# A fused layernorm, S4 convolution and NF4 gated MLP: the inverse transform of the S4 kernel with 8 products in place of 12

## The chip, the cores and the metric

The kernel runs on one core of one Trainium2 chip. A core has a tensor engine (PE, with its weight loads shown apart as PEld), a vector engine (VectorE, DVE), a scalar engine (ScalarE, ACT), GpSimd (POOL) and a sync engine (SP) whose queue issues most of the transfers. The metric is the device time of one execution in microseconds, the median of several runs. A change below about 0.2% of this kernel's time is hard to tell from none.

## The reference, cut to what matters

The input x has 4 x 512 rows of 512 features. It is normalised by layernorm, and the output is x plus an S4 convolution of the normalised x plus a gated MLP of it whose weights are 4-bit codes with scales.

```python
xn = _layernorm(x, axis=-1)
x = x + _L0_attn_ref(xn, ...) + _L0_ffn_ref(xn, ...)

# in _L0_attn_ref -> _s4_kernel
Omega = jnp.exp(-2j * jnp.pi * (jnp.arange(L) / L))       # L = 512
...
at_roots = c * (k00 - k01 * (1.0 / (1.0 + k11)) * k10)
return jnp.fft.ifft(at_roots, L).real

# in _L0_attn_ref
y = jnp.fft.irfft(jnp.fft.rfft(u, n=n) * jnp.fft.rfft(K, n=n), n=n)[..., :L]
return y + D[0] * u
```

The change touches the last line of `_s4_kernel`: the real part of an inverse Fourier transform of 512 complex values, which gives the 512 taps of the convolution kernel K.

## The kernel before, in words

**Stages.** The rows come in four blocks (`tb`) of 512. The first stage loads x, normalises it, transposes it on PE and computes the first pair of gate and up products (lines 499 to 657, an order written out by hand for ScalarE, VectorE, PE and SP). Then, for each m from 1 to 13, the codes of 128 gate and 128 up columns are dequantised by ScalarE and VectorE (`dequant`, line 237), and `hidden` (line 439) multiplies them with the four blocks on PE: 24 matmuls of 512 columns for a block, 96 for an m, and then a silu on ScalarE (line 432), a gating multiply on VectorE (line 436) and a store by SP (line 437). Every f32 operand of these is split in three parts, so that three products replace one. In between, the S4 part is emitted: `s4_roots` (line 253) after m=2, `s4_toeplitz` (line 366) after m=3, and the convolution `conv` (line 446) of one block after each of m=5 to 8. The last stage, `down` (line 464), multiplies with the down weights, and adds and stores the result.

**The S4 part.** `s4_roots` evaluates the transfer function at the 512 roots. The roots are held as four residues of 128: root 4p + r is partition p, column r. The result is in three tiles of 128 x 4, `qr`, `qi` and `nqi` (real part, imaginary part, minus the imaginary part).

`s4_toeplitz` makes the inverse transform in two steps. The **twist** (lines 377 to 380) multiplies each residue's 128 values by a 128 x 128 table of cosines and sines (`al`, `be`, loaded at line 370) into a real and an imaginary matrix (`ar`, `ai`): four VectorE operations for a residue, 16 in all, each over 128 x 128. Then **the products** (line 388) multiply these, as stationary operands, with a table of cosines and sines `b` of that residue. The table is loaded at line 369 (two blocks of 128 columns for a residue, cosine and minus sine), and GpSimd (line 372) writes its negative beside it, so that four turns by a quarter are at hand. The PSUM tile `pm` has four sums of 128 columns: residue 0, residue 2, and two sums over residues 1 and 3 with different turns. They take 2 + 2 + 4 + 4 = 12 products of 128 x 128 by 128 x 128 in f32. VectorE copies `pm` out, and adds and subtracts the sums (lines 397 to 401) into `toep`, which GpSimd masks (line 402); it is split in three parts into `tp` (line 409), the moving operand of the convolution.

**Buffers.** `b` and `b1` (which holds `al`, `be`, `ar`, `ai`) are the two buffers of the tag "xt", used before by `s4_roots` and after by the convolution's and the last stage's blocks. `pm` is one of four PSUM slots of two banks, which the `hidden` products use in turn.

**Order.** After the hand-ordered first stage, a planner with its own cost estimates orders the instructions of each engine, by the order in which the code emits them and by when it takes their inputs to be ready. Engines then work their queues in order, and wait for one another by semaphores. ScalarE and VectorE instructions emitted up to m=3 are tied behind the first stage (lines 673 to 676).

Of the kernel before, what the change touches and what calls it, by code (L numbers as in the profile page):

```python
# [12 lines left out]
ALU = mybir.AluOpType  # L13
# [3 lines left out]
P = 128  # L17
# [4 lines left out]
L = 512  # L22
# [39 lines left out]
def layernorm_s4_nf4_glu_kernel(  # L62
# [8 lines left out]
    down_s: bass.AP,  # L71
    s4_cols: bass.AP,
    s4_row: bass.AP,
    trig: bass.AP,
    cos_col: bass.AP,
    dft: bass.AP,
# [3 lines left out]
    nc = tc.nc  # L80
    V, S, G, T = nc.vector, nc.scalar, nc.gpsimd, nc.tensor
# [5 lines left out]
    def bank2(name):  # L87
        return psum.tile([P, 2, 512], F32, tag="ps", name=name)

    f = lambda ap: ap.bitcast(F32)  # L90
# [14 lines left out]
    def split(dst, src):  # L105
        S.activation(dst[0], src, AF.Copy, scale=TRIM)  # L106
        V.tensor_tensor(dst[1], src, f(dst[0]), ALU.subtract)  # L107
        V.scalar_tensor_tensor(dst[2], f(dst[1]), -LAM, f(dst[0]), ALU.mult, ALU.add)  # L108
# [257 lines left out]
    def s4_toeplitz():  # L366
        qr, qi, nqi = roots["qr"], roots["qi"], roots["nqi"]
        b, b1 = (work.tile([P, 4, 512], F32, tag="xt", name=f"s4b{k}") for k in range(2))
        nc.sync.dma_start(b[:, 0:4, 0:256], dft)
        nc.sync.dma_start(b1[:, 0:2, :], twist)  # L370

        G.tensor_scalar(b[:, 0:4, 256:512], b[:, 0:4, 0:256], -1.0, None, ALU.mult)
        al, be, ar, ai = (b1[:, j, :] for j in range(4))
        for r4 in range(4):
            c = bass.ts(r4, P)
            o = slice(r4, r4 + 1)
            V.tensor_scalar(ar[:, c], al[:, c], qr[:, o], None, ALU.mult)
            V.scalar_tensor_tensor(ar[:, c], be[:, c], nqi[:, o], ar[:, c], ALU.mult, ALU.add)
            V.tensor_scalar(ai[:, c], al[:, c], qi[:, o], None, ALU.mult)
            V.scalar_tensor_tensor(ai[:, c], be[:, c], qr[:, o], ai[:, c], ALU.mult, ALU.add)  # L380


        pm = bank2("pm")[:, 0, :].rearrange("p (k q) -> p k q", k=4)
        for k, terms in enumerate((((0, 0),), ((2, 0),), ((1, 0), (3, 0)), ((1, 1), (3, 3)))):
            n = 2 * len(terms)
            for i, (r4, turn) in enumerate(terms):
                for part, lhsT in enumerate((ar, ai)):
                    T.matmul(  # L388
                        pm[:, k, :], lhsT[:, bass.ts(r4, P)],
                        b[:, r4, bass.ts((turn + part) % 4, P)],  # L390
                        start=(i == 0 and part == 0), stop=(2 * i + part == n - 1),
                    )
        toep = work.tile([P, L], F32, tag="h", name="toep", bufs=4)
        tk = toep.rearrange("p (k q) -> p k q", k=4)
        cd = b1[:, 0, 0:384].rearrange("p (k q) -> p k q", k=3)
        pq = b1[:, 1, 0:256].rearrange("p (k q) -> p k q", k=2)
        V.tensor_copy(cd, pm[:, 1:4, :])
        V.tensor_tensor(pq[:, 0, :], pm[:, 0, :], cd[:, 0, :], ALU.add)
        V.tensor_tensor(pq[:, 1, :], pm[:, 0, :], cd[:, 0, :], ALU.subtract)
        V.tensor_tensor(tk[:, 0:2, :], pq, cd[:, 1:3, :], ALU.add)  # L400
        V.tensor_tensor(tk[:, 2:4, :], pq, cd[:, 1:3, :], ALU.subtract)
        G.affine_select(
            out=toep[:, 0:P], in_=toep[:, 0:P], pattern=[[1, P]], compare_op=ALU.is_ge,
            fill=0.0, base=0, channel_multiplier=-1,
        )
        V.scalar_tensor_tensor(
            toep[:, 0:P], ident, row[:, 64:65], toep[:, 0:P], ALU.mult, ALU.add
        )
        split([tp[:, i, :] for i in range(3)], toep)
        return tp  # L410
# [89 lines left out]
    start = len(traced)  # L500
# [159 lines left out]
    for m in range(2, NMT - 2):  # L660
        wp[m + 1] = dequant(gu(m + 1))
        for tb in range(NTB):
            hidden(m, tb, wp[m])
        p = {2: 0, 4: 1, 5: 2, 7: 3, 8: 4, 10: 5, 11: 6}.get(m)
        if p is not None:
            down_weights(p)
        if m == 2:
            s4_roots()
        if m == 3:
            toep = s4_toeplitz()  # L670
        if 5 <= m < 9:
            conv(m - 5, toep)
        if m == 3:
            for ins in list(traced[end:]):
                if ins.engine in (S.engine, V.engine):
                    tc.add_manual_dep(ins, last[ins.engine].name, order, reason="after the first tile")
# [27 lines left out]
def _layouts(a):  # L704

    import numpy as np

    def gu_q(q):
        return np.asarray(q).reshape(NMT, P, NC, P).transpose(0, 3, 2, 1).reshape(NMT, P, 512)

    def gu_s(s):
        return (
            np.asarray(s).reshape(NMT, P, NC, 2).transpose(0, 3, 2, 1).reshape(2 * NMT, 512)
        )

    lam, p, q, vc, ct = (
        np.asarray(a[f"L0_attn_{n}_ri"]) for n in ("Lambda", "p", "q", "Vc", "Ct")
    )
    state = np.concatenate(
        [lam, p, ct.reshape(NS, 2), q, vc.reshape(NS, 2 * NS)], axis=1  # L720
    )
    row = [np.asarray(a[f"L0_attn_{n}"]).reshape(-1) for n in ("Bp", "D", "log_step")]

    lr = 4 * np.arange(P)[:, None] + np.arange(4)[None, :]
    half = np.pi * lr / L
    th = 2 * np.pi * ((lr[:, :, None] * np.arange(P)) % L) / L
    tw = np.pi * ((lr[:, :, None] * (1 - 2 * np.arange(P))) % (2 * L)) / L
    f = np.float32
    return {
        "x": np.asarray(a["L0_attn_u"]).reshape(NTOK, HD),  # L730
        "gate_q": gu_q(a["L0_ffn_gate_q"]),
        "up_q": gu_q(a["L0_ffn_up_q"]),
        "down_q": np.asarray(a["L0_ffn_down_q"]).reshape(HD, NMT, P).transpose(1, 2, 0),
        "gate_s": gu_s(a["L0_ffn_gate_absmax"]),
        "up_s": gu_s(a["L0_ffn_up_absmax"]),
        "down_s": np.asarray(a["L0_ffn_down_absmax"]).reshape(HD, 2 * NMT).transpose(1, 0),
        "s4_cols": np.tile(state, (2, 1)),
        "s4_row": np.concatenate(row)[None, :],
        "trig": np.stack([np.sin(half), np.cos(half)]).transpose(0, 2, 1).reshape(2, L).astype(f),
        "cos_col": np.cos(half).astype(f),  # L740
        "dft": np.concatenate([np.cos(th), -np.sin(th)], axis=2).astype(f),
        "twist": (np.stack([np.cos(tw), np.sin(tw)], axis=1) / L).reshape(P, 2, 512).astype(f),
    }


# [21 lines left out]
```

## Time and profile before

| | |
|---|---|
| Median of 3 runs | 521.77 us (521.66 to 521.78) |
| Profiled execution, own time | 521.76 us |
| its span, first to last instruction | 520.0 us |
| granted TensorE clock, mean | 1.000 |
| Transferred | 96.46 MB, mean 185 GB/s |
| Chain that ended last, by engine | PE 96%, DMA 3% |
| on it: gu (line 416), po (481), pc (454), pm (388), pss (322) | 54%, 29%, 6%, 1%, 0% |

Busy time of each engine by stage, from the trace (the S4 transform's products lie in the third row):

| Stretch, us | PE | PEld | DVE | ACT | POOL | DMA share |
|---|---|---|---|---|---|---|
| 46 to 89 (m=1, 2) | 43.0 | 35.6 | 36.4 | 36.6 | 3.1 | 0.41 |
| 91 to 112 (m=3) | 21.0 | 17.4 | 13.5 | 15.6 | 0.0 | 0.62 |
| 112 to 115 (pm) | 3.0 | 2.9 | 1.2 | 3.0 | 0.0 | 0.73 |
| 115 to 158 (m=4, 5) | 43.0 | 35.6 | 22.4 | 40.1 | 0.4 | 0.81 |
| 158 to 254 (conv, m=6 to 8) | 96.0 | 82.7 | 44.3 | 76.5 | 0.8 | 0.65 |
| 254 to 363 (m=9 to 13) | 109.0 | 90.3 | 30.0 | 25.4 | 7.7 | 0.56 |
| 363 to 516 (down) | 153.0 | 125.7 | 71.5 | 27.0 | 1.2 | 0.37 |

How to read it: the profile is of one execution. A row such as `L388 PE MATMUL pm<-s4b,s4b x24` names the line of the code, the engine, the operation, and the tile written and the tiles read; a count and times follow. PE's instructions are pipelined, so their durations overlap. In the chain of work that ended last, each piece begins where the piece that released it ends. The tile name `s4b` stands for both `b` and `b1`.

### The profile page before, as it was taken

The page shows a single profiled execution, that of the slowest core. Times are in us where ns is not written, and L with a number is a line of the kernel's source. Part 1 is how long each engine was busy: PE and PEld are TensorE (multiplying, and loading weights), DVE is VectorE, ACT ScalarE, POOL GpSimd, SP SyncE. Part 2 cuts the span into 40 slices and gives each one's busy share as a digit, 9 for nine tenths or more (in the row PEclk, how much of TensorE's full clock was granted, in tenths as well). Part 3 has the DMA queues.
Part 4 walks back from the last instruction along what each step waited for, and adds up shares of the span by engine and source line. Part 5 has one row for each costly group of instructions (what it writes and reads, how often), then busy time and mean ns, then how long its engine had stood idle before and what let it go on. Part 6 is the DMA issues. An engine that isn't in the chain of part 4 may idle for free.

```text
span 520.0 us, 6138 instructions
## 1 busy us (share of the span) xinstructions
PE 513.7 (99%) x2336; PEld 421.0 (81%) x2336; DVE 259.8 (50%) x353; ACT 264.0 (51%) x326; POOL 19.9 (4%) x34
## 2 busy tenths in 40 slices
PE   8999999999999999999999999999999999999996
PEld 8556888888888888888888888888888888888885
DVE  6989796756545464253522332113545536536412
ACT  7889599599889968895362211102212112121100
POOL 1210002000000000000000000112000000000000
PEclk9999999999999999999999999999999999999999
DMA  8914417849774877755644322699634534524102
GB/s 298 334 36 150 136 46 283 244 142 329 274 245 153 286 246 263 248 178 187 262 164 191 112 101 79 229 348 336 221 122 133 195 118 145 206 97 161 42 1 81
DMA packets 37231, 96.46 MB, mean 185 GB/s; under 512 B 4689, under 2 KB 5585, under 8 KB 34385
## 3 DMA queue, kind: packets, MB, share of 16 engines
q1 hardware_dynamic: 34320, 80.60, 45.2%
q0 software_dynamic: 2592, 15.21, 8.2%
q8 instruction: 18, 0.29, 0.2%
q10 hardware_dynamic: 288, 0.26, 0.2%
q14 instruction: 13, 0.10, 0.1%
HBM read 61.97 MB, written 34.08 MB: 185 GB/s over the span
## 4 chain that ended last, share of the span: by engine, by line
PE 96%; DMA 3%; DVE 0%; SPq 0%; issue 0%
PE gu L416 54%; PE po L481 29%; PE pc L454 6%; PE u L424 3%; PE g L424 2%; DMA q_g1u<-in_up_q_dram 1%; DMA sc_g0u<-in_up_s_dram 1%; PE pt L168 1%; DMA q_g0u<-in_gate_q_dram 1%; PE pm L388 1%; PE pss L322 0%; DVE xo L488 0%; DVE q_g0u L540 0%; SPq L204 0%; SPq L211 0%
## 5 line engine op out<-in xcount | busy, mean ns | idle before, releaser
L481 PE MATMUL po<-wdt,hp 128*128 128x512 f32 x672 | 153.0, 390 | 0.0
L481 PEld LDWEIGHTS po<-wdt,hp 128*128 128x128 f32 x672 | 125.9, 188 | 27.0 <-DVE xo L488 0.9
L436 DVE SCALAR_TENSOR_TENSOR h<-gu,h 128x512 f32<-128x512 f32 x52 | 35.8, 689 | 108.9 <-ACT h L432 108.8
L106 ACT ACTIVATE hp<-hr 128x1024 fp32r<-128x1024 f32 x28 | 29.7, 1060 | 105.2 <-PE po L481 101.3
L432 ACT ACTIVATE h<-gu 128x512 f32<-128x512 f32 x52 | 30.6, 589 | 92.8 <-PE gu L416 92.8
L107 DVE TENSOR_TENSOR hp<-hr,hp 128x1024 fp32r<-128x1024 f32 x28 | 34.3, 1225 | 62.7 <-ACT hp L106 62.7
L108 DVE SCALAR_TENSOR_TENSOR hp<-hp 128x1024 fp32r<-128x1024 f32 x28 | 34.2, 1223 | 0.9
L454 PE MATMUL pc<-tp,xeT 128*128 128x512 f32 (+1 forms) x64 | 20.7, 323 | 0.0
L454 PE MATMUL pc<-tp,xlT 128*128 128x512 f32 (+1 forms) x64 | 20.6, 322 | 0.0
L454 PE MATMUL pc<-tp,xhT 128*128 128x512 f32 (+1 forms) x64 | 20.3, 318 | 0.0
L488 DVE SCALAR_TENSOR_TENSOR xo<-po,xo 128x512 f32<-128x512 f32 x16 | 10.8, 688 | 18.1 <-PE po L481 18.1
L424 PE MATMUL g<-xf,q_g0u 128*128 128x512 f32 (+1 forms) x40 | 14.7, 509 | 0.6 <-ACT xf L171 0.6
L424 PE MATMUL u<-xf,q_g0u 128*128 128x512 f32 x32 | 15.0, 596 | 0.3 <-DVE q_g0u L540 0.3
L424 PEld LDWEIGHTS g<-xf,q_g0u 128*128 128x128 f32 x40 | 7.4, 190 | 7.1 <-issue 4.8
L454 PEld LDWEIGHTS pc<-tp,xhT 128*128 128x128 f32 x64 | 12.2, 190 | 0.8
L454 PEld LDWEIGHTS pc<-tp,xlT 128*128 128x128 f32 x64 | 12.1, 189 | 0.8
L454 PEld LDWEIGHTS pc<-tp,xeT 128*128 128x128 f32 x64 | 12.1, 189 | 0.6
L460 DVE SCALAR_TENSOR_TENSOR xr<-pc,xr 128x1024 f32<-128x1024 f32 x8 | 9.8, 1219 | 5.2 <-PE pc L454 5.2
L142 DVE BATCH_NORM_STATS2 st<-x 128x6 f32<-128x512 f32 x16 | 10.9, 679 | 3.0 <-DMA x<-in_x_dram 3.0
L219 ACT ACTIVATE q_g0u<-q_g0u 128x256 f32<-128x256 f32 (+1 forms) x32 | 10.3, 407 | 1.4 <-DMA q_g0u<-in_gate_q_dram 1.4
L472 POOL DMA_DIRECT2D xo<-rd x4 | 2.3, 585 | 225.3 <-DMA rd<-xr 118.6
L690 POOL DMA_DIRECT2D wdt<-wdd x14 | 7.3, 528 | 94.2 <-issue 94.0
(278 smaller groups left out, 969.2 us busy)
## 6 DMA issues: line engine op xcount, KB each, us to landing
hd<-h SPq DMA_DIRECT2D x56, 256.0 KB, 2.9
hr<-hd SPq DMA_DIRECT2D x28, 512.0 KB, 3.4
wdt<-wdd POOLq DMA_DIRECT2D x7, 1024.0 KB, 6.9
xr<-in_x_dram SPq DMA_DIRECT2D x4, 1024.0 KB, 7.2
rd<-xr SPq DMA_DIRECT2D x4, 1024.0 KB, 4.9
xo<-rd POOLq DMA_DIRECT2D x4, 1024.0 KB, 7.0
out_dram<-xo SPq DMA_DIRECT2D x16, 256.0 KB, 3.4
wdt<-wdd POOLq DMA_DIRECT2D x7, 512.0 KB, 7.7
```

What stands on the lines that cost most here:

```text
L106: S.activation(dst[0], src, AF.Copy, scale=TRIM)
L107: V.tensor_tensor(dst[1], src, f(dst[0]), ALU.subtract)
L108: V.scalar_tensor_tensor(dst[2], f(dst[1]), -LAM, f(dst[0]), ALU.mult, ALU.add)
L142: V.bn_stats(st[:, j, :], xs[tb][:, j, :])
L219: S.activation(w, w if j else w.bitcast(I32), AF.Prelu, scale=scale, bias=bias, alpha=slope)
L416: T.matmul(ps[:, k, :], wp[:, part, k, bass.ts(c, P)], xT[tb][part][:, :, c, :], start=(part == 0 and c == 0), stop=(part == 2 and c == NC ...
L424: T.matmul(ps[:, j.start * P : j.stop * P], w[:, bass.ts(c, P)], xf[tb].rearrange("p j (c q) -> p j c q", c=NC)[:, j, c, :], start=(c == 0 ...
L432: S.activation(h, pg, AF.Silu, scale=unit)
L436: V.scalar_tensor_tensor(h, pu, unit, h, ALU.mult, ALU.mult)
L454: T.matmul(po[:, k, i * P : HD], xT[tb][part][:, jj + k, i, :], toep[:, part, 0 : HD - i * P], start=(i == 0 and part == 0), stop=(i == NC ...
L481: T.matmul(po[j], hp[:, part, k, bass.ts(j, P)], wd(p, part, k), start=(p == 0 and k == 0 and part == 0), stop=(p == NPR - 1 and k == 1 an ...
L488: V.scalar_tensor_tensor(o, po[j], OUT, o, ALU.mult, ALU.add)
```

## The change

Residue 3 is the complex conjugate partner of residue 1: root 4p + 3 reversed in p is 512 - (4p + 1). The tables on the host are laid out anew, so that column 3 holds residue 3 in reversed order, with the sine part of its twist negated. The twist of residue 3 then adds onto the matrices of residue 1 (`to` is the block 1 for r4 = 3), with the signs of a conjugate, in place of writing matrices of its own. With that, the sums over residues 1 and 3 become products of one matrix: `pm` takes 2 + 2 + 2 + 2 = 8 products. The table `b` of residue 3 is neither loaded nor negated, and the third quarter turn isn't needed any more: the load and GpSimd's multiply go over three residues instead of four. The arithmetic count of the twist stays at 16 operations; two of them change from a multiply to a multiply with an added tile.

```diff
-        nc.sync.dma_start(b[:, 0:4, 0:256], dft)
+        nc.sync.dma_start(b[:, 0:3, 0:256], dft)
         nc.sync.dma_start(b1[:, 0:2, :], twist)
 
-        G.tensor_scalar(b[:, 0:4, 256:512], b[:, 0:4, 0:256], -1.0, None, ALU.mult)
+        G.tensor_scalar(b[:, 0:3, 256:512], b[:, 0:3, 0:256], -1.0, None, ALU.mult)
         al, be, ar, ai = (b1[:, j, :] for j in range(4))
         for r4 in range(4):
+            to = bass.ts((0, 1, 2, 1)[r4], P)
             c = bass.ts(r4, P)
             o = slice(r4, r4 + 1)
-            V.tensor_scalar(ar[:, c], al[:, c], qr[:, o], None, ALU.mult)
-            V.scalar_tensor_tensor(ar[:, c], be[:, c], nqi[:, o], ar[:, c], ALU.mult, ALU.add)
-            V.tensor_scalar(ai[:, c], al[:, c], qi[:, o], None, ALU.mult)
-            V.scalar_tensor_tensor(ai[:, c], be[:, c], qr[:, o], ai[:, c], ALU.mult, ALU.add)
+            for dst, s1, s2 in (
+                ((ar, qr, nqi), (ai, qi, qr)) if r4 < 3 else ((ar, qr, qi), (ai, nqi, qr))
+            ):
+                if r4 < 3:
+                    V.tensor_scalar(dst[:, to], al[:, c], s1[:, o], None, ALU.mult)
+                else:
+                    V.scalar_tensor_tensor(
+                        dst[:, to], al[:, c], s1[:, o], dst[:, to], ALU.mult, ALU.add
+                    )
+                V.scalar_tensor_tensor(
+                    dst[:, to], be[:, c], s2[:, o], dst[:, to], ALU.mult, ALU.add
+                )
 
         pm = bank2("pm")[:, 0, :].rearrange("p (k q) -> p k q", k=4)
-        for k, terms in enumerate((((0, 0),), ((2, 0),), ((1, 0), (3, 0)), ((1, 1), (3, 3)))):
-            n = 2 * len(terms)
-            for i, (r4, turn) in enumerate(terms):
-                for part, lhsT in enumerate((ar, ai)):
-                    T.matmul(
-                        pm[:, k, :], lhsT[:, bass.ts(r4, P)],
-                        b[:, r4, bass.ts((turn + part) % 4, P)],
-                        start=(i == 0 and part == 0), stop=(2 * i + part == n - 1),
-                    )
+        for k, (r4, turn) in enumerate(((0, 0), (2, 0), (1, 0), (1, 1))):
+            for part, lhsT in enumerate((ar, ai)):
+                T.matmul(
+                    pm[:, k, :], lhsT[:, bass.ts(r4, P)], b[:, r4, bass.ts(turn + part, P)],
+                    start=(part == 0), stop=(part == 1),
+                )
...
     lr = 4 * np.arange(P)[:, None] + np.arange(4)[None, :]
+    lr[:, 3] = lr[::-1, 3]
...
+    tw = np.stack([np.cos(tw), np.sin(tw)], axis=1) / L
+    tw[:, 1, 3] *= -1.0
...
-        "dft": np.concatenate([np.cos(th), -np.sin(th)], axis=2).astype(f),
-        "twist": (np.stack([np.cos(tw), np.sin(tw)], axis=1) / L).reshape(P, 2, 512).astype(f),
+        "dft": np.concatenate([np.cos(th), -np.sin(th)], axis=2)[:, :3].astype(f),
+        "twist": tw.reshape(P, 2, 512).astype(f),
```

## The prediction

> **What bounds the kernel now.** I read the page's busy shares first, then the chain of work that ended last in order of time, then the waits of the tensor engine, then the single instructions around the changed lines. The busy shares of the page:
>
> ```profile
> PE 513.7 (99%) x2336; PEld 421.0 (81%) x2336; DVE 259.8 (50%) x353; ACT 264.0 (51%) x326; POOL 19.9 (4%) x34
> ...
> PEclk9999999999999999999999999999999999999999
> ```
>
> PE is busy nearly throughout, at full granted clock. The Trainium skill ("Perfetto Trace Analysis", section "Identifying the Most-Contended Engine") warns against reading this as a bound: matmul busy time says little of the distance to the roofline, and the share of the weight loads is the better measure. That speaks against the change. By the 81% of PEld, a fifth of the time might be gaps that take up any saving, and the sum would be 521.77 us again. So the chain has to decide:
>
> ```profile
> 16.53 0.69 DVE q_g0u L540
> ...
> 45.93 43.56 PE gu L416 x192
> 89.50 0.79 PE pss L322 x8
> 90.29 21.92 PE gu L416 x96
> 112.21 2.68 PE pm L388 x24
> 114.89 43.54 PE gu L416 x192
> 158.42 7.62 PE pc L454 x48
> ...
> 363.22 152.87 PE po L481 x672
> ```
>
> Columns are start, length, what. From 17.26 us to 516.10 us every piece is PE, each begins where the one before it ends, and no wait for a DMA or another engine lies between. The waits of PE alone confirm it:
>
> ```profile
> PE warm L532 <- POOL ident masks.py:199: 1.4, 1, 1.4
> PE g L424 <- ACT xf L171: 0.6, 1, 0.6
> PE u L424 <- DVE q_g0u L540: 0.3, 1, 0.3
> ```
>
> All three belong to the first tile, before 46 us. So the 19% without a weight load are stretches in which a 512-column product streams longer than its load, not idle time, and the row is taken over the rule: what leaves PE's queue leaves the end. The transform (tile pm, line 388) is on the chain with 2.68 us, 0.5%.
>
> **What the change removes.** The code has 12 products of 128 columns; the trace has 24 pairs of weight load and matmul for them, two for each f32 product. Eight remain, so 16 pairs, and 8 leave. What is one worth? The duration of a record is the wrong number:
>
> ```profile
> L388 PEld LDWEIGHTS pm<-s4b,s4b x24: 187/192/192, 111.8 to 114.5; 128*128 128x128 f32 x24
> L388 PE MATMUL pm<-s4b,s4b x24: 270/275/275, 112.0 to 114.6; 128*128 128x128 f32 x24
> ```
>
> 8 x 275 ns would be 2.2 us, but 24 x 275 ns is 6.6 us and the stage lasts 2.68: they overlap. What counts is the distance from start to start. In the timeline of PE:
>
> ```profile
> 112.05 2.84 PE L388 MATMUL pm<-s4b,s4b 128*128 128x128 f32 x24
> 114.64 1.17 PE L416 MATMUL gu<-xhT,wp_g4u 128*128 128x512 f32 x4
> ```
>
> The first of 24 starts at 112.05, the last ends at 112.05 + 2.84 = 114.89, so starts at 114.89 - 0.275 = 114.615: 23 distances in 2.565 us, 111.5 ns each. The chain gives 2.68 / 24 = 111.7 ns. The starts of the loads give (114.5 - 111.82) / 23 = 116.5 ns, an upper end, because their first distance is stretched by the long product in front of pm.
>
> The skill ("TensorE: Matmul & The Clock Gate", section "Back-to-back issue gap") would make it smaller: a warm gap of N / 2.4 + 2.5 ns, 55.8 ns for N = 128, or about 81 ns in a sustained stream of loads and matmuls. Its estimates are 8 x 55.8 = 0.45 us and 8 x 81 = 0.65 us. The row is this very instruction in f32 and stands at 111.5, so it decides: **8 x 111.6 = 0.89 us** off PE. I keep 0.45 and 8 x 116.5 = 0.93 for the range.
>
> **What it adds or moves elsewhere.** Two of VectorE's 16 operations of the twist change kind: for residue 3 the first of each pair becomes a multiply-add onto residue 1.
>
> ```profile
> L377 DVE TENSOR_SCALAR s4b<-s4b,qr x4: 278/278/286, 95.4 to 98.7; 128x128 f32<-128x128 f32 x4
> L378 DVE SCALAR_TENSOR_TENSOR s4b<-s4b,nqi x4: 339/342/344, 96.0 to 99.2; 128x128 f32<-128x128 f32 x4
> ...
> L372 POOL TENSOR_SCALAR s4b<-s4b x1: 3079/3079/3079, 84.3 to 84.3; 128x1024 f32<-128x1024 f32 x1
> ```
>
> 2 x (342 - 278) = 0.13 us. The last four operations now also build on each other's output, in two chains of two. The nearest row is this line itself, where a multiply-add already follows the product it accumulates onto; starts lie 0.2 to 0.34 us apart there, so another 0 to 0.3 us. The block now ends at 99.76 + 0.35 = 100.11 us and pm starts at 112.05: 11.9 us of cover, filled by the products of m=3. Take 0. Were the cover gone, the price would be 0.13 to 0.43 us. Behind the block on VectorE is the gating multiply of line 436 at 102.94, after 2.83 us of idle time in which it waits for ScalarE; that idle time takes the delay too.
>
> GpSimd negates 768 columns in place of 1024: 3.08 x 3/4 = 2.31 us, ending about 86.6 in place of 87.4. That is 25 us ahead of pm: 0. The load of the cosine table shrinks from 512 to 384 KB; it is issued on SP at 80.22 and lands 3.9 us later, so it too is hidden by 25 us or more. Behind it on SP is the load of gate codes for m=5 at 80.93, wanted by ScalarE at 97: 0 either way. The number of transfers stays, and none is moved past another by the diff. The host-side reordering of residue 3 changes contents, not sizes.
>
> **What is late next.** After pm everything on PE comes 0.89 us sooner, so all that PE consumes must have that much to spare. The weights of m=4 are ready at 93.25 + 1.21 = 94.5 us and first used at 114.64: 20 us. Those of m=5 have 24 us (112.5 against 136.5), and the later ones more. The Toeplitz parts are ready at 119.36 + 0.69 = 120.05 and first used at 158.3: 38 us. They will come hardly sooner, because the copy out of pm (114.93) stands behind a gating multiply that starts at 114.33 once ScalarE has delivered, whenever pm ends; the cover is ample all the same. PSUM has four slots: that of the first m=4 product is read out by 122.65 and wanted again at 136.5, 14 us. From 254 us on the other engines wait for PE, and the waits move with it.
>
> **The sum.** Against the profiled execution's own 521.76 us (span 520.0, 1.76 us around it): 520.0 - 0.89 + 1.76 = 520.87 us. The runs' median is 0.01 higher: **520.88 us**, or -0.17%. A measurement of this kernel can tell about 0.2%, 1.04 us, from no change, so this is a real gain that lies inside that band.
>
> **Rivals.**
>
> A, the sum above: 520.88, its own range 520.7 to 521.2, which takes in the skill's 81 ns (521.1). Chance 0.66.
>
> B, the saving is lost in part or whole: the twin gap figure of 55.8 ns holds, giving 521.3, or PE finds a wait later that was just covered, giving up to 521.77. For it: ScalarE is busy 40.1 of the 43 us from 115 to 158, so an order that is slightly other could use up time there. Against it: the margins of 14 us and more just listed. Chance 0.08.
>
> C, more than 1.04 us comes off. For it: the first 17.26 us of the chain are DMA landings of the first codes and scales, the one part not paced by PE; a program of other tables may see these land 0.15 us or more sooner, and that passes whole to the end. Against it: the three runs shown agree within 0.12 us, and those transfers are the same. About 520.65. Chance 0.16. (The full 2.2 us of the record durations, 519.6, I exclude by the overlap.)
>
> D, slower. The order of instructions after the first tile is made by a planner with costs of its own, and it plans anew. The mechanism is the place of pm in PE's queue. Now it follows the last product of m=3 at 112.05, while its operands are complete at 100.11. A planner that counts pm cheaper may put it earlier. In front of the third group of m=3 (101.17) the operands are still in time. In front of the second group (95.73) PE, which works in order, would stand for 100.1 - 95.7 = 4.4 us with everything behind it, and 4.4 - 0.89 makes 525.3 us. It decides from a place before 98.2 us, where the wait exceeds 0.89 + 1.04 us. Against it: pss and pm both stand exactly where the code emits them, after all products of m=2 and of m=3. Chance 0.10.
>
> **How the numbers follow.** Slower is D: 0.10. Faster by over 0.2% is C: 0.16. Within 0.2% is A and B, 0.66 + 0.08 = 0.74. The predicted time is A's. The range 520.55 to 521.5 holds A, nearly all of C (0.93 us and a start-up 0.3 us shorter gives 520.54) and B up to the smaller gap with 0.2 us of spread; it leaves out D, the far part of B and a little of C, under 2 in 10. All mass but D lies at or below today's time.
>
> **What would show it.** Right: 16 records of pm at 111 to 112 ns from start to start, a piece of about 1.79 us in the chain, no new wait of PE behind 46 us, ten multiply-adds and six multiplies in VectorE's block with its end near 100.2 to 100.5 us, and the pieces after pm of equal length to now. Wrong: pieces of gu, pc or po that are longer or broken by a wait, pm in another place than behind the m=3 products, or a first PE piece that does not start at 17.26 us.

## The result, and the profile after

The changed kernel takes 520.89 us (median of 21 runs, 520.57 to 521.22) against 521.78 us before (21 runs): ratio 0.9983, 95% interval 0.9977 to 0.9989. The gain of 0.89 us, 0.17%, is clear of the noise of so many runs, and lies inside the 0.2% band. Forecast were 520.88 us and a chance of 0.74 for that band.

The page of the changed kernel, its busy shares (all lines after line 70 of the code have moved by 1 to 12):

```profile
PE 512.8 (99%) x2328; PEld 419.8 (81%) x2328; DVE 259.9 (50%) x353; ACT 264.5 (51%) x326; POOL 19.4 (4%) x34
```

Eight records fewer on PE and 0.9 us less busy time; VectorE and ScalarE as before. The chain that ended last, in order of time (start, length, what):

```profile
16.59 0.70 DVE q_g0u L549
...
46.01 43.55 PE gu L425 x192
89.56 0.79 PE pss L323 x8
90.35 21.92 PE gu L425 x96
112.27 1.78 PE pm L398 x16
114.06 43.54 PE gu L425 x192
157.59 7.62 PE pc L463 x48
...
362.39 152.87 PE po L490 x672
```

The pm piece went from 2.68 us with 24 records to 1.78 us with 16: 0.90 us less. Every other piece of PE has the length that it had, to 0.01 us, and still each begins where the last ended. Down to the products of the last stage the chain is 363.22 - 362.39 = 0.83 us ahead; the missing 0.07 us are the start-up, where PE's first piece began at 17.34 us instead of 17.26. The profiled execution went from 521.76 to 520.90 us.

PE's waits in the changed kernel:

```profile
PE warm L541 <- POOL ident masks.py:199: 1.4, 1, 1.4
PE u L433 <- DVE q_g0u L549: 0.7, 1, 0.7
PE g L433 <- ACT xf L172: 0.3, 1, 0.3
```

No new wait: all are those of the first tile. Around the transform the other engines did shift. These are the rows of the tiles of the transform in the changed kernel (count, least, median and greatest ns, first and last start):

```profile
L398 PE MATMUL pm<-s4b,s4b x16: 270/275/275, 112.1 to 113.8; 128*128 128x128 f32 x16
L390 DVE SCALAR_TENSOR_TENSOR s4b<-s4b,qr x4: 347/347/350, 97.1 to 100.6; 128x128 f32<-128x128 f32 x4
...
L373 POOL TENSOR_SCALAR s4b<-s4b x1: 2145/2145/2145, 85.7 to 85.7; 128x768 f32<-128x768 f32 x1
```

The twist ends at 100.59 + 0.35 = 100.94 us (before: 100.11), 11 us ahead of pm.

### The profile page after: what moved, and what is told of

Its sections match the earlier page's. It is cut to its first block, busy times and chain, and to the rows that moved or that the text cites. A ratio compares the mean times of both kernels' runs of the same rounds, so it can differ in the third digit from the quotient of the medians.

```text
span 519.2 us, 6118 instructions
## 1 busy us (share of the span) xinstructions
PE 512.8 (99%) x2328; PEld 419.8 (81%) x2328; DVE 259.9 (50%) x353; ACT 264.5 (51%) x326; POOL 19.4 (4%) x34
## 4 chain that ended last, share of the span: by engine, by line
PE 96%; DMA 2%; DVE 1%; SPq 0%; issue 0%; DVEq 0%
PE gu L425 55%; PE po L490 29%; PE pc L463 6%; PE u L433 3%; PE g L433 2%; DMA x<-in_x_dram 1%; PE pt L169 1%; DMA q_g0u<-in_gate_q_dram 1%; DVE st L143 0%; PE pm L398 0%; SPq L212 0%; DVE x L154 0%; PE pss L323 0%; DVE mv L144 0%; DVE q_g0u L549 0%; DVE xo L497 0%
## 5 line engine op out<-in xcount | busy, mean ns | idle before, releaser
L433 PEld LDWEIGHTS u<-xf,q_g0u 128*128 128x128 f32 x32 | 5.8, 190 | 6.6 <-issue 5.7
```

Source lines behind the costliest of these rows:

```text
L433: T.matmul(ps[:, j.start * P : j.stop * P], w[:, bass.ts(c, P)], xf[tb].rearrange("p j (c q) -> p j c q", c=NC)[:, j, c, :], start=(c == 0 ...
```

## The experiments

All times are medians; each run's before was taken on the same chip and lay between 521.76 and 521.84 us. My theory is the prediction's: PE never waits, so a product costs its place in PE's queue, two records at 111.6 ns, and nothing else in the change touches the time. The rivals: R1, the gain comes from the rest of the change; R2, a record costs the gap that the prediction took from the Trainium skill (55.8 or 81 ns); R3, slack somewhere takes part up.

**One part alone.** First the products without the rest: in the kernel before, residue 3's four products are left out.

```diff
-        for k, terms in enumerate((((0, 0),), ((2, 0),), ((1, 0), (3, 0)), ((1, 1), (3, 3)))):
+        for k, terms in enumerate((((0, 0),), ((2, 0),), ((1, 0),), ((1, 1),))):
```

> The kernel before with the four products of residue 3 left out (its twist, its tables and the larger GpSimd multiply stay; the inverse transform lacks residue 3). Theory (each f32 product is two records of weight load and matmul at 111.6 ns on a PE that never waits): -0.89 us against before, about 520.89, and the pm piece of the chain 1.78 us. Rival R1 (the gain of the change came from the smaller tables, the shorter GpSimd multiply or the other twist): no gain, about 521.78.

Measured: 520.91 us (20 runs), ratio 0.9984 (0.9977 to 0.9990). The whole gain is there. Then the rest without the saving: in the changed kernel the four products of residue 1 are issued twice.

```diff
-        for k, (r4, turn) in enumerate(((0, 0), (2, 0), (1, 0), (1, 1))):
+        for k, (r4, turn) in ((0, (0, 0)), (1, (2, 0)), (2, (1, 0)), (2, (1, 0)), (3, (1, 1)), (3, (1, 1))):
```

> The changed kernel with each of the four products of residue 1 issued twice, the second time over the first (12 products as before; everything else as changed; the output is unchanged). Theory: the price of the four products comes back, +0.89 us against the changed kernel, about 521.78, that is nothing against before. Rival R1 (the gain came from the rest of the change): stays at about 520.89.

Measured: 521.76 us (13 runs), ratio 1.0000 (0.9992 to 1.0009). The chain of this run:

```profile
90.30 21.92 PE gu L425 x96
112.22 2.68 PE pm L398 x24
114.90 43.54 PE gu L425 x192
```

With 24 records pm is back at 2.68 us and the time back at that of before, although the tables, the twist, the GpSimd multiply and nearly all of the planner's order are those of the change. R1 falls: what the smaller tables and the other twist are worth can't be told from nothing (the interval leaves about 0.4 us either way), and in the chain no other piece of PE differs from before by more than 0.01 us.

**The price of a record.** The changed kernel with its products three times over.

```diff
-        for k, (r4, turn) in enumerate(((0, 0), (2, 0), (1, 0), (1, 1))):
+        for k, (r4, turn) in 3 * list(enumerate(((0, 0), (2, 0), (1, 0), (1, 1)))):
```

> The changed kernel with its 8 products issued three times over (16 products more, 32 records, output unchanged). Theory: 32 x 111.6 ns = +3.57 us against the changed kernel, about 524.46 us. Rival R2 (the price is the skill's gap for 128 columns): +1.79 us at 55.8 ns (522.7) or +2.59 us at 81 ns (523.5). Rival R3 (another engine has slack that is used up when PE gets longer, or PE idles somewhere and takes part of it up): clearly less than 3.5 us.

Measured: 524.58 us (5 runs), +3.69 against 520.89. The chain:

```profile
112.39 5.36 PE pm L398 x48
117.74 43.54 PE gu L425 x192
```

5.36 / 48 = 111.7 ns a record; pm grew by 3.58 us. Another 0.09 us are a later start-up (17.43 us instead of 17.34); the last hundredths I don't assign. R2 (522.7 or 523.5) falls, and R3 too: 3.6 us more of PE work pass to the end undiminished.

What makes it 111.7 ns? The same 16 additional products, with half the columns:

```diff
+        for k, (r4, turn) in 2 * list(enumerate(((0, 0), (2, 0), (1, 0), (1, 1)))):
+            for part, lhsT in enumerate((ar, ai)):
+                T.matmul(
+                    pm[:, k, 0:64], lhsT[:, bass.ts(r4, P)],
+                    b[:, r4, (turn + part) * P : (turn + part) * P + 64],
+                    start=(part == 0), stop=(part == 1),
+                )
```

> The changed kernel with 16 products more as in the run with the products thrice, but these 16 with a moving operand of 64 columns in place of 128 (output unchanged). It tells what sets the 111.6 ns. If the columns streamed set it: half of it, some 56 ns for a record, +1.8 us, about 522.7. If the 128 x 128 weight load sets it, as the products of pss in the trace of before hint, with 8 columns and still about 100 ns a record: 100 to 112 ns a record, +3.2 to +3.6 us, 524.1 to 524.5.

Measured: 524.54 us (5 runs), the same as with whole columns. From this run's rows of pm (the label of the shape covers the rows of line 398 alone):

```profile
L398 PE MATMUL pm<-s4b,s4b x32: 217/275/275, 112.0 to 115.4; 128*128 128x64 f32 x32
```

and from its chain, the half products first and the whole ones behind them:

```profile
112.14 3.52 PE pm L398 x32
115.66 1.84 PE pm L405 x16
```

The 32 records of 64 columns take 3.52 us, 110 ns each; with the 16 whole ones behind them the two pieces are again 5.36 us. Half the streaming bought nothing. That is what the pss row of before had shown, too:

```profile
L322 PE MATMUL pss<-vv,s4a x8: 170/256/256, 89.3 to 90.0; 128*128 128x8 f32 x8
```

These are 8 records of 8 columns in a piece of 0.79 us, 99 ns each. The quotients 99 and 110 are low only because the second of these short records starts 25 and 55 ns behind the first; from there on the starts lie 110 to 112 ns apart in both rows, as they do with 128 columns. So a short record's price is not that of its columns. What all these records share is a load of 128 x 128 weights. The Trainium skill's page "TensorE: Matmul & The Clock Gate" gives P / 1.2 ns for the load of P columns in its section "LDWEIGHTS", which makes an estimate of 107 ns for 128 columns, close to the 111.6 of the trace. That it is the load, and not a fixed price of a record that happens to be as large, is not shown: no run changes the size of the stationary operand. The gap that I weighed in the prediction, from another section of that page, is not the price of this shape.

The opposite cut leaves the columns and takes away loads: the two sums of residue 1 side by side, 2 products of 256 columns in place of 4 of 128.

```diff
-        for k, (r4, turn) in enumerate(((0, 0), (2, 0), (1, 0), (1, 1))):
+        for k, r4, w in ((0, 0, 1), (1, 2, 1), (2, 1, 2)):
             for part, lhsT in enumerate((ar, ai)):
                 T.matmul(
-                    pm[:, k, :], lhsT[:, bass.ts(r4, P)], b[:, r4, bass.ts(turn + part, P)],
+                    pm[:, k : k + w, :], lhsT[:, bass.ts(r4, P)],
+                    b[:, r4, part * P : (part + w) * P],
```

> The changed kernel with the two sums of residue 1 made side by side: two products of 256 columns in place of four of 128 (4 weight loads fewer, the same columns; output unchanged). If the weight load alone set the price: -4 x 107 ns = -0.43 us, about 520.46. If an f32 record also needs its columns' time, which the 512-column f32 products of the first tile put at 429 ns / 512 = 0.84 ns a column, that is 107 ns for 128 and 214 ns for 256: 4 x 214 in place of 8 x 111.6 ns, -0.04 us, about 520.85, no change that can be told.

Measured: 520.93 us (18 runs), no change that can be told. The pm row of this run:

```profile
L398 PE MATMUL pm<-s4b,s4b x12: 270/275/382, 112.0 to 113.6; 128*128 128x128 f32 x8, 128*128 128x256 f32 x4
```

and its piece in the chain:

```profile
112.19 1.76 PE pm L398 x12
```

1.76 - 8 x 0.1116 = 0.87 us for the four wide records, 217 ns each: about twice the price for twice the columns. So both limits meet at about 128 columns. Below, a record costs about 111.6 ns whatever its columns; above, these f32 records take 0.84 to 0.85 ns a column (217 / 256 here; 429 / 512 in the first tile, whose pieces of 4 take 1.72 us).

**Case D by hand.** The transform is emitted behind the first group of m=3, and PE's second group is tied behind pm.

```diff
+        if m == 3:
+            hidden(m, 0, wp[m])
+            toep = s4_toeplitz()
+            mm = [ins for ins in traced[end:] if ins.engine == T.engine]
+            first = len(traced)
-        for tb in range(NTB):
+        for tb in range(1 if m == 3 else 0, NTB):
             hidden(m, tb, wp[m])
+        if m == 3:
+            later = [ins for ins in traced[first:] if ins.engine == T.engine]
+            tc.add_manual_dep(later[0], mm[-1].name, order, reason="pm ahead")
...
-        if m == 3:
-            toep = s4_toeplitz()
```

> The changed kernel with the transform emitted behind the first group of m=3, and PE's queue tied so that the second group stands behind pm (case D of the prediction, made by hand). Theory (PE works in order and has no slack to take a wait up): in the trace of after the twist ends at 100.94 us and the second group starts at 95.79, so PE stands about 5.1 us and the time is 520.89 + 5.1 = about 526.0; 525.3 if the twist ends as early as before. Rival R3 (later idle time of PE takes it up): well under 524.

Measured: 527.56 us (4 runs), 1.6 us above what I expected. PE's timeline in this run (start, length, what, and in brackets the idle time ahead of it):

```profile
98.00 0.80 PE L398 MATMUL pm<-s4b,s4b 128*128 128x128 f32 x4 [2.20 <-ACT h L441]
100.38 3.13 PE L398 MATMUL pm<-s4b,s4b 128*128 128x128 f32 x12 [1.58 <-DVE s4b L390]
103.16 2.05 PE L425 MATMUL gu<-xhT,wp_g3u 128*128 128x512 f32 x4
```

and the busy times by stretch (length; busy us and instructions of PE, PEld, DVE, ACT, POOL; granted clock; DMA share; GB/s):

```profile
95.00:100.00 5.00, 1.60 (x8) 0.88 (x6) 4.93 (x25) 4.68 (x6) 0.00 (x0) 0.85 0.60 174
100.00:103.00 3.00, 2.62 (x11) 2.50 (x12) 2.78 (x8) 0.71 (x1) 0.00 (x0) 0.50 0.85 219
103.00:106.00 3.00, 3.00 (x11) 2.47 (x10) 2.20 (x7) 2.25 (x4) 0.41 (x1) 0.62 0.68 214
```

PE stood for 2.20 + 1.58 = 3.8 us, and the granted clock fell to 0.50 and 0.62 in the stretches behind it. Four products of 512 columns took 2.05 us there, where the first four behind pm take 1.17 in the changed kernel. In stretches of half a microsecond the clock is 1.00 up to 98.0 us, 0.97 from 98.0 to 98.5, and 0.50 from there to 105.0. I had priced the wait alone.

In the profiled execution (528.05 us) the sum comes out so. From the end of the first group (98.00 - 2.20 = 95.80 us) to that of pm (103.51) 7.7 us pass, 5.9 more than pm takes at full clock: 3.8 us of waits, and 0.80 + 3.13 - 1.79 = 2.1 us by which pm's own products are slower. (Part of these 2.1 us would have been a wait otherwise, since the twist ends at 101.64 us.) The 264 products behind pm lose another 0.9 us: 60.79 us here, 59.89 in the run that follows.

To tell the wait from the clock, the gap is filled with useless transposes:

```diff
             hidden(m, 0, wp[m])
+            n0 = len(traced)
+            fill = bank2("fill")
+            for _ in range(44):
+                T.transpose(fill[:, 0, 0:P], ident, ident)
             toep = s4_toeplitz()
...
+            for one, two in zip(q, q[1:]):
+                tc.add_manual_dep(two, one.name, order, reason="filled")
```

> The run with pm early once more, with 44 transposes of the identity matrix put on PE in front of pm (about 109 ns each, 4.8 us of otherwise useless work where PE stood still). Theory of the 1.6 us by which that run exceeded its expectation: the wait of PE let its granted clock fall to 0.5 until about 105 us, and pm and the first products behind it ran at half speed. Then the fill keeps the clock at 1.0, pm ends some 0.9 us behind the twist, and the time falls from 527.56 to about 525.9, although PE has 4.8 us more to do. Rival R5 (the 1.6 us are the wait itself and the clock costs nothing): 527.5 or more.

Measured: 526.24 us (4 runs). Its chain:

```profile
95.94 4.81 PE fill L676 x44
100.75 1.79 PE pm L398 x16
102.54 59.89 PE gu L425 x264
```

and its stretches:

```profile
95.00:100.00 5.00, 5.00 (x44) 4.79 (x43) 4.94 (x27) 4.08 (x5) 0.00 (x0) 1.00 0.58 189
100.00:103.00 3.00, 3.00 (x26) 2.92 (x25) 2.56 (x6) 1.77 (x2) 0.00 (x0) 1.00 0.81 238
```

44 transposes that nobody needs made the kernel 1.32 us faster than waiting did. The clock stays at 1.00 and pm keeps its 1.79 us, so R5 falls. The fill ends at 100.75, so its 4.81 us are now the loss. The 0.3 us between 525.9 and 526.24 I find in the tail: from the last VectorE piece's end to the end of the span it is 524.5 - 520.22 - 0.69 = 3.6 us here and 519.2 - 515.29 - 0.69 = 3.2 in the changed kernel. It is not the last store: its packets are done 1.7 us behind that piece in both. The run with pm early, without the fill, has 3.6 us too. What makes the closing instructions longer is open.

**A further step.** If only PE's queue counts, the other conjugate pairs can be folded as well. Residues 0 and 2 are partners of themselves; each becomes one real contraction of 128 rows (64 real, 64 imaginary parts), so 1 + 1 + 2 + 2 = 6 products remain. The values at the partner roots come through two small transfers that swap the halves of the partitions. Its core, the host tables aside:

```diff
+        for h in range(2):
+            nc.sync.dma_start(qsw[bass.ts(h, 64)], qri[bass.ts(1 - h, 64)])
...
+            (m0, ((0, qr, 0), (1, qi, 0), (2, sr, 0), (3, si, 0))),
+            (m2, ((4, qr, 2), (5, qi, 2), (6, sr, 2), (7, si, 2))),
...
-        for k, (r4, turn) in enumerate(((0, 0), (2, 0), (1, 0), (1, 1))):
+        for k, terms in enumerate((((m0, 0),), ((m2, 1),), ((ar, 2), (ai, 3)), ((ar, 3), (ai, 4)))):
```

> A further step on the changed kernel: the conjugate pairs of residues 0 and 2 are folded too, each as one contraction over 64 real and 64 imaginary rows, so that pm takes 1 + 1 + 2 + 2 = 6 products of 128 columns (output unchanged). For it the roots' values go through two small transfers that swap the halves of the partitions (SP, behind the roots), the twist's table grows from 512 to 768 KB, VectorE stays at 16 operations. Theory: 4 records fewer on PE, -0.45 us against the changed kernel, about 520.44, as long as the swapped values arrive before the twist is needed (11 us of cover in front of pm). Rival R4 (a transfer of 2 us and more in the twist's chain, and a wait on SP's queue, cost time somewhere): 520.9 or more.

Measured: 520.46 us (9 runs), ratio to before 0.9975 (0.9965 to 0.9984). Because the step to the changed kernel is small, both ran once more on one chip.

> The changed kernel itself, on one chip with the run of six products that follows, so that the two can be compared directly: 520.89.

> The kernel with six products again, beside the changed one: 4 records fewer, -0.45 us, about 520.45, if the first run's 520.46 (9 runs) was no luck; no gain over the changed kernel if it was.

Measured: 520.92 us (21 runs) and 520.43 us (10 runs), a step of 0.49 us where 0.45 was expected. The rows of the swapped values in the six-product kernel's first run:

```profile
L367 SPq DMA_DIRECT2D qsw<-qri x2: 493/544/596, 96.3 to 96.9; - x2
...
L394 DVE SCALAR_TENSOR_TENSOR s4b<-s4b,qsw x4: 348/349/349, 100.0 to 100.8; 128x128 f32<-128x128 f32 x4
```

and its chain:

```profile
112.37 1.34 PE pm L399 x12
113.71 43.54 PE gu L426 x192
```

The swaps are issued from 96.3 us, land 2.0 to 2.3 us later, and VectorE uses them from 100.0, 12 us ahead of pm. So R4 falls: the cover in front of pm, which hid the change's own additions, hides a transfer chain too. pm is 1.34 us. This version beats both kernels, by 1.3 to 1.4 us the one before and by 0.4 to 0.5 us the changed one.

## Why the prediction was right, point by point

**What bounds the kernel.** Right. The chain had no gap, so the advice of the Trainium skill ("Perfetto Trace Analysis", section "Identifying the Most-Contended Engine") to judge the distance to the roofline by the share of the weight loads, 81% here, was rightly put aside for this question. With products added and products taken away the time followed PE's queue: -4, +16 and -2 products of the changed transform moved pm by -0.90, +3.58 and -0.44 us, and the medians by -0.89, +3.69 and -0.43 to -0.49.

**The price of a record.** Right: 0.89 us predicted, 0.90 measured in the chain, 111.7 ns a record in the longest run. Taking the start-to-start distance, not the record's duration of 275 ns and not the page's gap, was the choice that decided. That the median as well lies within 0.01 us of the forecast is luck: the interval of the gain is 0.57 to 1.20 us, and the start-up alone differs by 0.27 us between profiles. What sets the distance, the prediction left open; the half columns and the wide products show a floor of about 111.6 ns, which fits the weight load, with the columns' time close behind it.

**What is added elsewhere.** Its sum, nothing, is right as far as can be told: the run with all of the change but the saving is at 1.0000 (0.9992 to 1.0009). Its details were off where cover made it harmless. The twist ended at 100.94 us where I had 100.2 to 100.5, mainly because the root values came later: qi starts at 96.13 instead of 95.32. The planner had ordered ScalarE otherwise, so that the multiply of m=4's codes, which VectorE does ahead of the roots, came at 89.97 instead of 88.66. GpSimd's multiply took 2.15 us, not 2.31, and began later, at 85.72, so that it ended at 87.87, not 86.6. And the Toeplitz parts were ready at 121.08 + 0.68 = 121.76 us, 1.7 us later than before instead of hardly sooner: a dequantising multiply now stands between the copy out of pm (114.27) and the sums (115.87), and two more ahead of the split. They are first used at 157.6, so 36 us of cover remain.

**The rivals.** B did not happen; nothing absorbed the saving. C's mechanism, a start-up that lands otherwise, is real but small and went the other way: 17.34 us in the profile of after (a first PE piece that does not start at 17.26 us is one of the signs of being wrong that the prediction named), and 17.17 to 17.44 in the experiments, 0.27 us from end to end. C needed it 0.15 us sooner than 17.26, and none of these profiles shows that, so its chance of 0.16 was rather high. D did not happen: in PE's queue the products stand in the same place in both programs, while 17 of VectorE's 353 instructions, 15 of ScalarE's 325 and 12 of SP's 257 in the two traces stand in another place of their queues or are of another kind. Its mechanism is real, but its price was too low. Made by hand it costs 6.7 us over the changed kernel where the prediction's 4.4 us, and the 5.1 us of the expectation, priced the wait alone; the half clock behind it was left out.

## What to carry to other kernels

When the chain shows one engine without a gap, price an edit by the start-to-start distance of that very instruction in that very shape, and count everything on other engines at nothing only after naming the cover; here both held within the noise. On PE look first at whether the columns or the floor under a record (probably its weight load) set the distance: cutting columns below 128 bought nothing here, cutting products did. And the cover is a resource: the 11 us in front of pm took two transfers of over 2 us for free and so bought another 0.43 to 0.49 us.

## What the runs showed of the hardware

A product in f32 with a 128 x 128 stationary operand shows as two records. From start to start a record in a row of its kind takes 110 to 112 ns with 8, 64 and 128 columns, 217 ns with 256 and 429 ns with 512.

PE standing for 3.8 us, broken by 0.8 us of work, brought its granted clock down to 0.50 for the products behind it, for 6.8 us (98.5 to 105.3), although PE worked without a break from 100.38 us on. 4.8 us of filler transposes in the same place kept it at 1.00 and were 1.32 us faster than idling. The Trainium skill's account of the clock gate ("TensorE: Matmul & The Clock Gate", section "What's actually happening") has the half clock after an idle window of about 3.4 us. The half is what the run shows, the length is not: the longest stand without work was 2.20 us, and the clock fell 2.7 us after PE had stopped, when it had just begun to work again. For the wait of 4 to 5 us that I forecast, in a stream that had been busy for nearly 80, the page would have spoken of the half clock, and I had not applied it.
